# First rows by tiles in two queues, fewer idle products, queries before the first values, and transfers of the early sums and next rows issued at other places

## The chip, the core and the metric

The kernel runs on one core of a Trainium2 chip. The time is device microseconds (us) from start to end of one execution; lower is better. A core has TensorE (PE, products; PEld is its weight load), VectorE (DVE), ScalarE (ACT), GpSimd (POOL) and SyncE (SP, here used to issue DMA transfers). Each engine takes its instructions in order, and they wait for each other through semaphores. Transfers issued by SP and by ACT run on the same 16 DMA engines.

## What is computed

A transformer block on x of 8 sequences, 512 tokens, 256 features, all in float32: attention with 16 heads of 128 (4 groups of keys and values, causal), then a mixture of 64 experts, of which each token takes 6, and a shared expert. Cut to what matters:

```python
def reference(x, wq, bq, wkv, bkv, wo, gate_w, w_gate, w_up, w_down, sh_gate, sh_up, sh_down):
    def attention(x):                                  # x: 8 x 512 x 256
        q = (x @ wq + bq) + pe                         # 4 groups x 4 heads x 128
        k, v = split(x @ wkv + bkv); k = k + pe        # 4 groups x 128 each
        probs = softmax(causal(q @ k.T / sqrt(128)))
        return (probs @ v) @ wo
    def ffn(h):                                        # 4096 tokens, 64 experts, width 176
        w, i = top_k(softmax(h @ gate_w.T), 6)
        y = sum over the 6 of w * ((silu(h @ w_gate[i]) * (h @ w_up[i])) @ w_down[i])
            # of each expert only its first 64 tokens, in the order of tokens
        return y + (silu(h @ sh_gate.T) * (h @ sh_up.T)) @ sh_down.T
    x = x + layernorm(attention(layernorm(x)))
    return x + layernorm(ffn(layernorm(x)))
```

## The kernel before

**Steps.** The main loop runs over k = 0 to 127, a sequence b = k // 16 and a head s = k % 16, and is a pipeline of heads written out by hand: the order of every engine's instructions is the order in which the program calls them. In step k TensorE makes the scores of head k (`scores`, four row tiles of 128, L328), the output product of head k-3 (`project`, L407), the queries of head k+1 (`queries`, L315) and the mixing of head k-2 with the values (`mix`, pav, L390). DVE takes the scores out of PSUM with their mask and row extremum (L332), ACT exponentiates (L335), POOL divides by the row's sum (L345). The scores' PSUM pool has three buffers (`ps_s`, tag "s"), so the fourth tile of a head waits until DVE has evicted the first.

**Turning of the probabilities.** For head k-1, in step k, DVE transposes blocks of 32 x 32 into eb (L361), SP stores them in four transfers to a scratch ex_d (L366), and then reads them back in turned order as et with one transfer of 640 KB (L371). The read waits in SP's queue until the four stores have landed. `turned` also runs, between the stores and the et read, whatever functions the list `readings` holds (L133 to L135 put the turned normalized rows there).

**Sequences.** `prepare(b)` gives the work on a sequence's rows in units: load (`load_x`, L167, one transfer of 512 KB by SP), statistics (`scales`, st_a, L78 to L88, with POOL's power), normalizing (xn, L107), transposing, keys of four groups (pk), values of four row tiles (pv). For sequence 0 the units are called before the loop: keys of group 0, values of tile 0, queries of head 0, and the others in the first steps. For the next sequence the load is called in step s = 6, behind the et read of that step and what a finished sequence stores, the statistics at the end of s = 7, and so on. x has two buffers: rows of b+1 go where those of b-1 were, whose last reader is the normalizing for the feed forward part (xg, L107, step s = 6 in `feed_forward(b-1)`), after a store of them to x1_d (L825, step s = 5).

**Start.** SP loads x of sequence 0, then wkv, biases, the positions, wq in four parts, wo and the shared expert's weights. TensorE makes WARM = 28 products of an identity (L174) before the first transposes (L120).

**Experts and end.** The first five sequences (EARLY) are gathered by expert and run on the way (weights loaded by ACT's queue). In the last steps, `finish_early` finishes their rows: for each of the five, one after the other every four half-steps, it loads the two partial sums y0 and y1 (512 KB each, from y_d, issued by ACT, L711), loads x1 (512 KB, by SP, L726), adds y1 to y0 on POOL (L716), takes statistics (`output`, L78 to L88), scales on ACT (L98), adds x1 on POOL (L702) and stores (L704). The main loop calls it once after the queries and once at a step's end. `last_part` does sequence 7's second half, mixed with what is left of sequence 6 and of `finish_early`. Experts with too many late tokens for the on-the-way buffers are run in a loop after it (L1084), whose count is computed by the kernel; in the profiled execution it was passed without a turn. Behind the loop stand the last products of sequence 7 (L965), which add one late pair's output to PSUM, and `last_output`: statistics, subtraction (L970), scaling and residual (L972), stores (L974).

Each transfer of SP's and ACT's queues ends on one of eight semaphores, taken in turn in the program's order; a transfer waits, on its issuing engine, until the one that had its semaphore before has landed.

Of the kernel before, what the change touches and what calls it, by code (L numbers as in the profile page):

```python
# [11 lines left out]
F32 = mybir.dt.float32  # L12
# [7 lines left out]
P = 128  # L20
B, T, E = 8, 512, 256
NT = B * T
NI = T // P
# [3 lines left out]
NC = E // P  # L27
G, QPG, D = 4, 4, 128
# [7 lines left out]
NEG = -3.0e38  # L36
BIG = 3.0e38
ROW = E + NX
WARM = 28
EARLY = 5  # L40
ET_ROWS = EARLY * T
LROW = ROW + NX
# [2 lines left out]
def sandwich_kernel(ctx, tc, x, wq, bq_t, wkv, bk_t, bv, wo, gate_wt, w_gate, w_up, w_down,  # L45
                    sh_gate_t, sh_up_t, sh_down_t, pe_t, out):
    nc = tc.nc
# [55 lines left out]
    def rows_of(d, first):  # L103
        return d[first : first + T, :].rearrange("(i p) e -> p i e", p=P)
# [19 lines left out]
    readings = []  # L124
# [21 lines left out]
    with ExitStack() as part:  # L146
# [3 lines left out]
        wpool = pool("weights", 1)  # L150
# [9 lines left out]
        def load(ap, shape, name):  # L160
            t = wpool.tile(shape, F32, tag=name, name=name)
            nc.sync.dma_start(out=t, in_=ap)
            return t

        def load_x(b):
            t = p2.tile([P, NI, E], F32, tag="x", name=f"x_{b}")
            nc.sync.dma_start(out=t, in_=x[ts(b, T), :].rearrange("(i p) e -> p i e", p=P))  # L167
            return t

        x_first = load_x(0)  # L170
# [1 line left out]
        warm = ps_s.tile([P, T], F32, tag="s", name="warm")  # L172
        for n in range(WARM):
            nc.tensor.matmul(warm[:, :P], lhsT=ident, rhs=ident, start=True, stop=True)  # L174
        wkv_sb = load(wkv.rearrange("(c p) (g k d) -> p c g k d", p=P, g=G, k=2), [P, NC, G, 2, D], "wkv_sb")
        bk_sb = load(bk_t, [D, G], "bk_sb")
        bq_sb = load(bq_t, [D, NH], "bq_sb")
        pe_sb = load(pe_t, [D, T], "pe_sb")
# [64 lines left out]
        NK = B * NH  # L243
# [309 lines left out]
        table, pairs = {}, {}  # L553
# [153 lines left out]
        def finish(b, tags):  # L707

            ys = [q.tile([P, NI, E], F32, tag=tag, name=f"y{n}_{b}") for n, (q, tag) in enumerate(tags[:2])]
            for k in range(2):  # L710
                nc.scalar.dma_start(out=ys[k], in_=rows_of(y_d, k * (ET_ROWS + CAP) + b * T))  # L711
            yield
            yield
            yield
            x1 = residual(b, *tags[2])
            nc.gpsimd.tensor_add(ys[0], ys[0], ys[1])  # L716
            yield
            yield
            for n, _ in enumerate(output(b, ys[0], x1)):
                yield  # L720
                if n == 1:
                    yield

        def residual(b, q, tag):
            x1 = q.tile([P, NI, E], F32, tag=tag, name=f"x1_{b}")
            nc.sync.dma_start(out=x1, in_=rows_of(x1_d, b * T))  # L726
            return x1
# [168 lines left out]
        def last_part(before, spare):  # L896


            b, xt, sums = B - 1, seqs[B - 1]["x"], po.pop(B - 1)
# [57 lines left out]
            l["part"](py, 0)  # L957
            output6()
            down("late")
            return py, xt, gt, pairs["late"]["dd"]  # L960

        def last_output(py, x1, gt, dd):
            b = B - 1
            for i in range(NI):
                nc.tensor.matmul(py[i // 2][:, i % 2, :], lhsT=gt[:, ts(i, P)], rhs=dd, start=False, stop=True,  # L965
                                 skip_group_check=True)
# [12 lines left out]
        def finish_early():  # L979
            rows = [finish(b, EARLY_TAGS + [[(p1, "xn"), (p2, "xnt")][b % 2]]) for b in range(EARLY)]  # L980
            yield

            for t in range(4 * EARLY + 5):
                for b in range(EARLY):
                    if 0 <= t - 4 * b < 9:
                        next(rows[b])
                yield

# [1 line left out]
        units = list(prepare(0))  # L990
        rest = {"0B": units[9:10], "0D": units[10:11], "1B": units[11:12], "1D": units[5:6], "2B": units[6:7],
                "3B": units[7:8]}
        for u in units[:5] + units[8:9]:
            u()
        queries(0)
        assert len(units) == 12
        behind, ahead = {}, iter(())
        routed, zeroing = experts(), zeros()
# [9 lines left out]
        for k in range(NK):  # L1008
            b, s = divmod(k, NH)
            active = k >= EARLY * NH + 14  # L1010
            scores(k, 0)
            scores(k, 1)
            if 0 <= k - 1 < NK - 2:
                turned(k - 1)
            if twice and not finishing:
# [17 lines left out]
            if finishing:  # L1033
                next(routed, None)
            side(s, "M")
            if s == 6 and b <= EARLY:
                ahead = prepare(b + 1)
                next(ahead)()
            if b <= EARLY and s == 8:
                next(ahead)()  # L1040
            if k >= 2:
# [24 lines left out]
            twice = active and k > EARLY * NH + NH  # L1066
            if twice and not finishing:
                next(routed, None)
            if finishing:
                next(routed, None)  # L1070
            if active and not finishing and "all" in pairs:
                routed, finishing = finish_early(), True
# [11 lines left out]
        with tc.For_i(0, table["rest"], 1) as n:  # L1084
# [17 lines left out]
            down("late")  # L1102
            for i in range(NI):
                nc.tensor.matmul(sums[i // 2][:, i % 2, :], lhsT=gts[-1][:, ts(i, P)], rhs=pairs["late"]["dd"],
                                 start=False, stop=False, skip_group_check=True)
# [62 lines left out]
```

## Time and profile before

| what | us |
|---|---|
| median of 3 runs (lowest, highest) | 1423.16 (1421.56, 1423.8) |
| the profiled execution | 1423.76 |
| its span, first to last instruction | 1422.0 |
| TensorE busy in the span | 1381.9 |
| TensorE waiting for a score tile's eviction by DVE | 10.9 (7 waits) |
| TensorE waiting for et | 5.5 (4 waits) |
| TensorE waiting at the loop before the last products | 2.9 |
| DVE waiting for x | 11.4 (5 waits) |
| mean granted TensorE clock | 0.996 of full |

How to read it: the span is what the trace covers; some 1.8 us of the execution lie around it. A row of the time line has its start, how long the group lasted, engine, line, operation, output and input tile, shape, number of instructions, and in brackets how long the engine stood idle before it and what ended that. A TensorE product in float32 is recorded as passes, two for each product of this kernel. "DMA x<-in_x" as a releaser is a transfer's landing. A wait for several semaphores is put down to the one that came last.

### The profile page before, as it was taken

The numbers are of one execution on the slowest core, as the hardware profiler recorded it, in microseconds if no ns is written. First come the engines' busy times: TensorE is split into PE (matmuls) and PEld (weight loads), VectorE is DVE, ScalarE is ACT, GpSimd is POOL, SyncE is SP. The second block draws the span as 40 slices with busy tenths as digits, with TensorE's granted clock in tenths as the row PEclk, the third lists the DMA queues.
The fourth block names the chain that finished last, engine by engine and source line by source line (L and its number), as shares of the span: only waits on it lengthen the run. The fifth ranks groups of instructions, "written<-read, shape, count | busy, mean of one in ns | idle before, by whom it ended". The sixth has DMA issues, their size and how long they took to land. (4 is left out here: it accounts for less than half of the span.)

```text
span 1422.0 us, 18479 instructions
## 1 busy us (share of the span) xinstructions
PE 1381.9 (97%) x5230; PEld 839.9 (59%) x5230; DVE 887.4 (62%) x3125; ACT 497.5 (35%) x1428; POOL 446.1 (31%) x710
## 2 busy tenths in 40 slices
PE   9999999999999999999999999999999999999996
PEld 5665665666556665666556665655555565555564
DVE  5565577656775576566775577566656545567545
ACT  2332344224342333234432344223343333434421
POOL 2232242213321242113221232124544444445521
PEclk9999999999999999999999999999999999999998
DMA  7675566446763566446663566349998789777711
GB/s 235 187 217 156 153 195 204 138 122 169 220 173 109 150 186 203 127 125 168 202 183 108 148 195 174 110 133 289 296 299 245 227 233 273 191 226 228 231 59 68
DMA packets 166934, 261.45 MB, mean 184 GB/s; under 512 B 17180, under 2 KB 141053, under 8 KB 166829
## 3 DMA queue, kind: packets, MB, share of 16 engines
q1 hardware_dynamic: 132013, 210.96, 50.8%
q10 hardware_dynamic: 28672, 39.85, 9.0%
q0 software_dynamic: 6144, 9.44, 3.4%
q8 instruction: 42, 0.69, 0.2%
q14 instruction: 63, 0.52, 0.1%
HBM read 148.25 MB, written 111.94 MB: 183 GB/s over the span
## 5 line engine op out<-in xcount | busy, mean ns | idle before, releaser
L345 POOL TENSOR_SCALAR e<-e,recip 128x128 f32<-128x128 f32 x508 | 268.4, 572 | 740.0 <-DVE recip L342 727.3
L335 ACT ACTIVATE e<-e,least 128x128 f32<-128x128 f32 (+3 forms) x512 | 285.6, 559 | 361.0 <-DVE least L332 349.0
L328 PE MATMUL psc<-kt,qt 128*128 128x128 f32 (+3 forms) x1024 | 304.8, 436 | 12.9 <-DVE least L332 10.9
L390 PE MATMUL pav<-et,v 128*128 128x512 f32 (+3 forms) x1024 | 298.3, 434 | 5.7 <-DMA et<-ex_d 5.5
L390 PEld LDWEIGHTS pav<-et,v 128*128 128x128 f32 x1024 | 194.2, 191 | 168.5 <-issue 119.3
L332 DVE CUSTOM_DVE_ANT_0 e<-psc,mask 128x128 f32<-128x128 f32 (+3 forms) x512 | 232.5, 479 | 61.3 <-PE psc L328 52.7
L407 PE MATMUL po<-wo_sb,ao 128*128 128x256 f32 x1024 | 243.7, 381 | 2.3 <-ACT ao L110 1.8
L315 PE MATMUL pq<-xnt,wq_sb 128*128 128x512 f32 x512 | 241.1, 593 | 0.3 <-ACT sc L434 0.3
L407 PEld LDWEIGHTS po<-wo_sb,ao 128*128 128x128 f32 x1024 | 193.0, 190 | 74.5 <-issue 41.7
L361 DVE STREAM_TRANSPOSE eb<-e 128x128 f32<-128x128 f32 x756 | 227.8, 364 | 6.9 <-DMA ex_d<-eb 5.9
L110 ACT COPY ao<-pav 128x512 f32<-128x512 f32 x128 | 74.7, 583 | 430.4 <-PE pav L390 412.4
L328 PEld LDWEIGHTS psc<-kt,qt 128*128 128x128 f32 x1024 | 162.2, 191 | 78.0 <-DVE least L332 31.3
L318 DVE SCALAR_TENSOR_TENSOR qt<-pq,bq_sb,pe_sb 128x512 f32<-128x512 f32 x128 | 95.5, 746 | 109.2 <-PE pq L315 109.2
L315 PEld LDWEIGHTS pq<-xnt,wq_sb 128*128 128x128 f32 x512 | 95.9, 190 | 70.2 <-issue 64.0
L342 DVE RECIPROCAL recip<-total 128x4 f32<-128x4 f32 x128 | 22.8, 178 | 121.0 <-ACT e L335 121.0
L335 ACT ACTIVATION_READ_ACCUMULATOR e<-e,least 128x1 f32 x512 | 95.7, 187 | 0.0
L632 POOL DMA_INDIRECT y_d<-dd,idx x32 | 50.8, 1588 | 93.1 <-DMA y_d<-dd,idx 27.5
L285 PE MATMUL pk<-xnt,wkv_sb 128*128 128x512 f32 x128 | 59.3, 594 | 0.2 <-ACT xnt L110 0.2
L296 PE MATMUL pv<-wkv_sb,xnt 128*128 128x512 f32 x128 | 58.1, 592 | 0.0
L298 DVE TENSOR_TENSOR v<-pv,bv_sb 128x512 f32<-128x512 f32 x32 | 22.1, 690 | 45.8 <-PE pv L296 45.8
L288 DVE SCALAR_TENSOR_TENSOR kt<-pk,bk_sb,pe_sb 128x512 f32<-128x512 f32 x32 | 24.0, 750 | 41.4 <-PE pk L285 41.4
L595 PE MATMUL pgu<-wgu,gxt 128*64 128x352 f32 x256 | 43.6, 461 | 0.7 <-issue 0.7
(201 smaller groups left out, 1074.9 us busy)
## 6 DMA issues: line engine op xcount, KB each, us to landing
ex_d<-eb SPq DMA_DIRECT2D x504, 160.0 KB
et<-ex_d SPq DMA_DIRECT2D x126, 640.0 KB
wgu<-in_w_gate ACTq DMA_DIRECT2D x32, 352.0 KB
wgu<-in_w_up ACTq DMA_DIRECT2D x32, 352.0 KB
wd<-in_w_down ACTq DMA_DIRECT2D x32, 352.0 KB
y<-y_d ACTq DMA_DIRECT2D x10, 512.0 KB
x<-in_x SPq DMA_DIRECT2D x8, 512.0 KB
x_d<-x SPq DMA_DIRECT2D x7, 512.0 KB
```

Of the source, the lines that this page charges most:

```text
L110: nc.scalar.copy(dst, src)
L285: nc.tensor.matmul(pk, lhsT=wkv_sb[:, c, g, 0, :], rhs=s["xnt"][:, c, :], start=c == 0, stop=c == NC - 1)
L296: nc.tensor.matmul(pv, lhsT=s["xnt"][:, c, ts(i, P)], rhs=wkv_sb[:, c, :, 1, :], start=c == 0, stop=c == NC - 1)
L315: nc.tensor.matmul(pq, lhsT=wq_sb[h // QPG][:, c, ts(h % QPG, D)], rhs=seqs[b]["xnt"][:, c, :], start=c == 0, stop=c == NC - 1)
L318: nc.vector.scalar_tensor_tensor(qt, pq, bq_sb[:, h : h + 1], pe_sb, ALU.add, ALU.add)
L328: nc.tensor.matmul(psc[:, :w], lhsT=l["qt"][:, ts(i, P)], rhs=seqs[b]["kt"][h // QPG][:, :w], start=True, stop=True)
L332: nc.vector.tensor_tensor_reduce(out=e, in0=psc[:, :w], in1=mask[:, T - w :], scale=-1.0 / math.sqrt(D), scalar=BIG, op0=ALU.add, op1=ALU. ...
L335: nc.scalar.activation(e, e, AF.Exp, bias=l["least"][:, i : i + 1], scale=-1.0, accum_out=l["total"][:, i : i + 1])
L345: engine.tensor_scalar(e, e, recip[:, n : n + 1], 1.0, ALU.mult, ALU.mult)
L361: nc.vector.transpose(blocks.rearrange("p c j t -> p j c t"), l["e"][i][:, js[0] * P : (js[-1] + 1) * P].rearrange("p (j c t) -> p j c t", ...
L390: nc.tensor.matmul(pav[:, :, j:, :], lhsT=seqs[b]["v"][:, j, ts(g, D)], rhs=l["et"][:, :, AT[j] : AT[j] + NI - j, :], start=j == 0, stop=j ...
L407: nc.tensor.matmul(po[b][i // 2][:, i % 2, :], lhsT=ao[:, ts(i, P)], rhs=wo_sb[:, h, :], start=h == 0 and i % 2 == 0, stop=h == NH - 1, sk ...
```

## The change

- Sequence 0's x is loaded in four transfers of one row tile each, on SP and ACT in turn; wkv in two, one on SP and one on ACT. WARM is 14.
- The queries of head 0 are made before the values of tile 0.
- The load of the next sequence's rows goes through `readings`: in step s = 6 SP issues it between the ex_d stores and the et read of that step. It waits there for the x1_d store and for xg, which in the program's order stand before and after it.
- `finish`: y0 in one half-step, y1 in the next, x1 in the one after these; POOL's sum in four instructions, one a row tile; the store one half-step earlier. The last half-step's call at k = 127 is left out, so that what it did (scaling and adding of the fifth sequence) is done by `last_part`.
- The last products stand before the loop, in `last_part`.

```diff
-WARM = 28
+WARM = 14
         def load_x(b):
             t = p2.tile([P, NI, E], F32, tag="x", name=f"x_{b}")
-            nc.sync.dma_start(out=t, in_=x[ts(b, T), :].rearrange("(i p) e -> p i e", p=P))
+            rows = x[ts(b, T), :].rearrange("(i p) e -> p i e", p=P)
+            if b:
+                nc.sync.dma_start(out=t, in_=rows)
+                return t
+
+            for i in range(NI):
+                (nc.sync, nc.scalar)[i % 2].dma_start(out=t[:, i, :], in_=rows[:, i, :])
             return t
...
-        wkv_sb = load(wkv.rearrange("(c p) (g k d) -> p c g k d", p=P, g=G, k=2), [P, NC, G, 2, D], "wkv_sb")
+        wkv_sb = wpool.tile([P, NC, G, 2, D], F32, tag="wkv_sb", name="wkv_sb")
+        for c in range(NC):
+            (nc.sync, nc.scalar)[c].dma_start(out=wkv_sb[:, c], in_=wkv[ts(c, P), :].rearrange("p (g k d) -> p g k d", g=G, k=2))
...
             for k in range(2):
                 nc.scalar.dma_start(out=ys[k], in_=rows_of(y_d, k * (ET_ROWS + CAP) + b * T))
-            yield
-            yield
-            yield
+                yield
             x1 = residual(b, *tags[2])
-            nc.gpsimd.tensor_add(ys[0], ys[0], ys[1])
-            yield
-            yield
-            for n, _ in enumerate(output(b, ys[0], x1)):
-                yield
-                if n == 1:
-                    yield
+            yield
+            for i in range(NI):
+                nc.gpsimd.tensor_add(ys[0][:, i, :], ys[0][:, i, :], ys[1][:, i, :])
+            yield
+            yield
+            yield from output(b, ys[0], x1)
...
             down("late")
-            return py, xt, gt, pairs["late"]["dd"]
-
-        def last_output(py, x1, gt, dd):
+            for i in range(NI):
+                nc.tensor.matmul(py[i // 2][:, i % 2, :], lhsT=gt[:, ts(i, P)], rhs=pairs["late"]["dd"],
+                                 start=False, stop=True, skip_group_check=True)
+            return py, xt
+
+        def last_output(py, x1):
             b = B - 1
-            for i in range(NI):
-                nc.tensor.matmul(py[i // 2][:, i % 2, :], lhsT=gt[:, ts(i, P)], rhs=dd, start=False, stop=True,
-                                 skip_group_check=True)
...
-            for t in range(4 * EARLY + 5):
+            for t in range(4 * EARLY + 4):
                 for b in range(EARLY):
-                    if 0 <= t - 4 * b < 9:
+                    if 0 <= t - 4 * b < 8:
                         next(rows[b])
...
-        for u in units[:5] + units[8:9]:
+        for u in units[:5]:
             u()
         queries(0)
+        units[8]()
...
             scores(k, 1)
+            if s == 6 and b <= EARLY:
+                ahead = prepare(b + 1)
+                readings.append(next(ahead))
             if 0 <= k - 1 < NK - 2:
                 turned(k - 1)
...
-            if s == 6 and b <= EARLY:
-                ahead = prepare(b + 1)
-                next(ahead)()
...
-            if finishing:
+            if finishing and k < NK - 1:
                 next(routed, None)
```

In the loop behind, the same products of a further turn end with stop=True instead of False.

More of the change, by code (lines that the diff above doesn't have):

```diff
@@ L711, in finish @@
                 nc.scalar.dma_start(out=ys[k], in_=rows_of(y_d, k * (ET_ROWS + CAP) + b * T))
+                yield
+            x1 = residual(b, *tags[2])
+            yield
+            for i in range(NI):
+                nc.gpsimd.tensor_add(ys[0][:, i, :], ys[0][:, i, :], ys[1][:, i, :])
             yield
             yield
-            yield
-            x1 = residual(b, *tags[2])
-            nc.gpsimd.tensor_add(ys[0], ys[0], ys[1])
-            yield
-            yield
-            for n, _ in enumerate(output(b, ys[0], x1)):
-                yield
-                if n == 1:
-                    yield
+            yield from output(b, ys[0], x1)
         def residual(b, q, tag):
@@ L1104, in sandwich_kernel @@
                 nc.tensor.matmul(sums[i // 2][:, i % 2, :], lhsT=gts[-1][:, ts(i, P)], rhs=pairs["late"]["dd"],
-                                 start=False, stop=False, skip_group_check=True)
+                                 start=False, stop=True, skip_group_check=True)
             for b in range(EARLY, B - 1):
```

## The prediction

> **What bounds the kernel now.** I read the page first: which engine is full, and whether it is full all the time.
>
> ```profile
> PE 1381.9 (97%) x5230; PEld 839.9 (59%) x5230; DVE 887.4 (62%) x3125; ACT 497.5 (35%) x1428; POOL 446.1 (31%) x710
> ```
>
> TensorE is busy in 97% of the span, so a change can only win where TensorE stands still, where it works slowly, or at the two ends. The second view is who TensorE waited for (us in total, times, longest):
>
> ```profile
> PE psc L328 <- DVE least L332: 10.9, 7, 2.5
> PE pav L390 <- DMA et<-ex_d: 5.5, 4, 1.9
> PE py L965 <- SPq L1084: 2.9, 1, 2.9
> ...
> PE po L407 <- ACT ao L110: 1.8, 1, 1.8
> ```
>
> These are few, long waits, and asked by window they lie in known places: 6.91 us of the first row are four waits, one in each of the sequences 1 to 4 (TensorE stands still at 222.5, 379.0, 535.8 and 692.9 us for 1.46, 1.73, 1.62 and 2.10 us). The rest lies in the last 150 us. The third view is the time line of the start:
>
> ```profile
> 1.87 9.37 PE L174 MATMUL warm<-ident 128*128 128x128 f32 x56 [1.87 <-POOL ident masks.py:199]
> 4.87 1.41 DVE L78 BATCH_NORM_STATS2 st_a<-x 128x6 f32<-128x256 f32 x4 [2.40 <-DMA x<-in_x]
> 7.91 1.38 DVE L107 TENSOR_SCALAR xn<-x,mv_a,rs_a 128x256 f32<-128x256 f32 x4 [1.15 <-POOL rs_a L88]
> 11.08 1.04 PE L120 MATMUL pt_a<-ident,xn 128*128 128x128 f32 x8
> ...
> 18.61 2.43 PE L328 MATMUL psc<-kt,qt 128*128 128x128 f32 x8 [0.84 <-DVE qt L318]
> ```
>
> The rows are normalized at 9.29 us, but the idle products keep TensorE until 11.1: they are the bound there. The fourth is the same around one of the four waits, DVE and then SP:
>
> ```profile
> 210.44 1.84 DVE L107 TENSOR_SCALAR xg<-x,mv_f,rs_f 128x256 f32<-128x256 f32 x4
> 221.85 1.41 DVE L78 BATCH_NORM_STATS2 st_a<-x 128x6 f32<-128x256 f32 x4 [1.99 <-DMA x<-in_x]
> ```
> ```profile
> 213.53 0.34 SPq L371 DMA_DIRECT2D et<-ex_d  x1
> 216.16 0.46 SPq L167 DMA_DIRECT2D x<-in_x  x1
> ```
>
> The next rows are asked for at 216.16 and land at 221.8; DVE stands at their statistics for 1.99 us, the scores behind them are late in leaving PSUM, and TensorE stops.
>
> **Start.** (a) Each of the four x tiles has its own transfer. The last still lands near 4.84 (from 3.5 us on all 16 DMA engines are full in the trace, so a second queue adds no bandwidth), but three tiles' statistics are done by then: only one of four, 0.41 us, comes after it. Statistics end at about 5.25 instead of 6.28: 1.0 us. The chain behind (aggregates, POOL's power of 1.03 us, normalizing) then ends at about 8.25.
>
> (b) 14 products instead of 28. Here a rule speaks against the change. In the trace the 56 passes (two a product) have two speeds. The table by stretches, asked for line L174 alone, shows it in the count of passes (us, length, TensorE busy and passes, weight loads, granted clock, share and rate of the DMA; the clock has no record before 7.9 us, and 1.00 there is a default):
>
> ```profile
> 6.00:8.00 2.00, 2.00 (x12) 2.00 (x11) 1.00 1.07 371
> 8.00:10.00 2.00, 2.00 (x21) 2.00 (x20) 1.00 0.90 244
> ```
>
> A pass starts every 0.2125 us until 7.8 and every 0.111 us after. The Trainium skill (page "TensorE: Matmul & The Clock Gate", Part 1) says that the array runs at half clock until it was busy for one free-running window of about 3.4 us, and goes back after an idle one. The row agrees in kind, but took 6 us, since the first window had begun before the products. By the row, 28 slow passes last 1.87 + 28 x 0.2125 = 7.8 to 8.0 us, just to the rows' arrival and to the end of that window: the transposes follow at full speed, at 7.95 instead of 11.08 less one pass, so 3.1 us earlier, of which (a) is a condition. By the rule, with the window elsewhere, the half clock may last to 12.1, and the transposes, keys and part of the queries (3 to 4 us of work) take about 2 us more, some 0.4 of it behind the transfer below. I take the row and keep the 2 us for the range.
>
> (c) Queries before the values. The first scores waited 0.84 us for DVE's qt; now four passes of values (1.71 us) lie over that 0.75 us eviction: -0.84. But the queries need wq's first part, which lands at 11.46 us in the trace; the keys now end at 9.2 + 1.8 = 11.0, so TensorE waits about 0.4. The bytes ahead of wq are the same. Its issue now also waits for an x tile (a transfer takes over the semaphore of the one eight before it), at 4.5 instead of 3.9 us, while the engines are still full with wkv. Sum of the start: 3.1 + 0.84 - 0.4 = **3.5 us**, from 1.5 (half clock) to 4.2. ScalarE's three issues (1.4 us) come before its table load; it is first needed at 8.5.
>
> **Next rows.** The load goes ahead of the et read in SP's queue, and now waits there for the old rows' last reader, DVE's xg. That ends at 212.28, 368.78, 525.56 and 682.66; the et reads, which wait for the ex_d stores to land, are issued at 213.53, 369.48, 526.40 and 683.52. So the load fits into SP's own wait, 0.7 to 1.25 us before it ends, for 0.4 to 0.9 us of issue, and rows land about 3.9 us earlier than now; DVE wanted them 2.0 to 2.6 us earlier. All four TensorE waits go: **6.9 us**. Behind the load are et and through it the mixing two steps later: it has 0.79 to 1.65 us to spare at these four places (landing of et to pav's start), and 512 KB at the 370 GB/s of the start's trace take 1.4 us, most of them before et's own data would begin: 0.2 to 0.7 us late, inside the spare time. If half of it were not, 4 x 0.4 = 1.6 us come back. Sequences 0 and 5 had no such wait: nothing.
>
> **Last sequences.** (d) At the last step the fifth sum's four ScalarE scalings stood before ao:
>
> ```profile
> 1359.36 2.08 ACT L98 ACTIVATE y<-y,shift_y,rs_y 128x256 f32<-128x256 f32 x4 [2.37 <-POOL shift_y L697]
> 1361.34 0.56 ACT L110 COPY ao<-pav 128x512 f32<-128x512 f32 x1
> ```
>
> TensorE's 1.76 us wait for it goes. The scalings and POOL's four sums (2.77 us) come after the last head instead; POOL is then about 0.5 us late for rs_o, which DVE and the transposes wait for: net 1.2.
>
> (e) y0 and y1 (512 KB each) come half a step apart and x1 one step earlier. Now they come with an output store in one burst of 2 MB, and the ex_d stores behind them land late (issued from 1332.88, landed at 1342.16); two mixings wait 1.91 and 1.59 us for it. With half the burst these should land some 4 us earlier. But stores still wait for a semaphore that a y transfer holds, at new places, where other reads have 1.4 to 2.5 us to spare. Between a gain of 3.5 and as much of new waits I take +2.0, as the bytes in front are halved. y1 lands later, but POOL's sums follow at least 11 us after its new issue, and it took 7.0 to 10.2.
>
> (f) POOL's sum is cut into four (4 x 0.69 for 2.35 us). DVE met it once:
>
> ```profile
> 1288.29 2.34 POOL L716 TENSOR_TENSOR y<-y,y 128x1024 f32<-128x1024 f32 x1
> ```
> ```profile
> 1288.55 2.13 DVE L443 TENSOR_SCALAR xg<-sc,grecip 128x64 f32<-128x64 f32 x1
> ```
>
> Its sister rows take 0.24 us. "SBUF — State Buffer" of the Trainium skill (the single rule on the shared ports) has the pair locked for a whole instruction. Shorter locks let DVE in between, but three more such DVE instructions follow, each of which can meet the next piece: 0 to 1.9, I take 0.3. Sum of the last sequences: 1.2 + 2.0 + 0.3 = **3.5 us**, from -2 to 7.
>
> **End.** The last products stood behind the empty loop:
>
> ```profile
> 1407.30 0.37 ACT L110 COPY dd_late<-pd_late 128x256 f32<-128x256 f32 x1 [2.85 <-PE pd_late L621]
> ...
> 1410.21 3.27 PE L965 MATMUL py<-dd_late,gt 128*128 128x256 f32 x8 [2.95 <-SPq L1084]
> ...
> 1413.52 0.76 DVE L78 BATCH_NORM_STATS2 st_y<-py 128x6 f32<-128x256 f32 x2 [0.95 <-PE py L965]
> ```
>
> They now start at 1407.7 and take 1.99 us, as their like before (they ran at half clock after the pause: 3.27). The loop's exit is set by sequence 6's output landing at 1409.16 and leaves DVE free at 1409.9; with TensorE done at 1409.7 this moves to 1410.2. Four statistics of 0.41 us end at 1411.9 instead of 1414.28: **2.4 us**, 1.0 if every engine waits for TensorE's slow row of semaphore checks.
>
> **Sum.** 3.5 + 6.9 + 3.5 + 2.4 = 16.3 us. The profiled execution took 1423.76 (span 1422.0 and 1.8 around it), 0.6 over the median; the same 16.3 from the median of 1423.16 give **1406.9 us**.
>
> **Rivals.** (1) *Half clock at the start*: speaks for it the rule above and a fall to half clock elsewhere (the last products); against it that TensorE is busy from 1.87 to 8.9 without a break, two windows nearly. Start 1.5: 1408.9. (2) *The last sequences only exchange their waits*: for it the semaphore places, against it the halved burst. -1 instead of 3.5: about 1411.5. (3) *Slower*: SP stands at the next rows' load, because DVE is late with xg, and et and everything behind it in SP's queue are late, at five places (sequence 0's et has 1.70 us to spare). The other gains stay, so it decides only when et is late by 16.3/5 + 1.45 = 4.7 us at each, and gives more than 1426 at 5.3. For it: SP takes its instructions in order. Against it: xg ended 0.7 us or more before et's issue in all four. About 1427. (4) *No change*: TensorE's waits come back elsewhere, as the scores behind DVE. DVE is at 62%, and stood still for the time that is taken away: little for it.
>
> **How the numbers follow.** Forecast 0.63 (its own range 1402 to 1411), rival 1 0.12, rival 2 0.17, rival 3 0.04, rival 4 0.04. A measurement of this kernel tells about 0.2% (2.8 us) from no change. The first three are faster: 0.92; same 0.04; slower 0.04. The range from 1401 (ends of the gains: 4.2, 6.9, 7, 2.6, and a clock fall before the last 160 us avoided) to 1415 (1.5, 5.3, 0, 1.5) holds the first three.
>
> **What would show it.** Right: the transposes of the first rows near 8 us and scores near 14.8; no DVE wait for x after the first rows; no TensorE wait at the loop; last products of 2 us. Wrong: first keys at 0.43 us a pass doubled to 0.85, pav waiting for et of the heads 21, 37, 53, 69 (mixed two steps after), new pav waits after 1270 us, or ScalarE standing at a y1 issue.

## The result

The changed kernel takes **1412.18 us** (median of four runs, 1408.62 to 1414.8), the kernel before 1423.48 beside it: a ratio of **0.9919, 95% interval 0.9892 to 0.9946**. By the ratio it is faster by 11.5 us; the forecast was 16.3 us and 1406.9 us. The time lies inside the range of 1401 to 1415, but above the forecast's own 1402 to 1411 and near the 1411.5 of the second rival, whose reason is not what happened. That it lies inside is partly luck: the range was kept wide for half clock and for exchanged waits, and what came in their place was late weights at the start. A repetition on another occasion gave 1409.95 against 1424.3, ratio 0.9913 [0.9891, 0.9935].

The profiled execution took 1414.8 us (span 1413.1), the slowest of its four. Its page and its waits of TensorE (us in total, times, longest), to be held against the same two views of before:

```profile
PE 1380.6 (98%) x5202; PEld 836.6 (59%) x5202; DVE 889.3 (63%) x3125; ACT 497.9 (35%) x1428; POOL 448.4 (32%) x725
```
```profile
PE ptx L592 <- DVE ht L113: 3.0, 1, 3.0
PE psc L336 <- DVE least L340: 2.9, 3, 1.4
PE pav L398 <- DMA et<-ex_d: 2.9, 3, 1.8
PE psg L764 <- DMA xt<-exr_d: 2.4, 4, 0.8
PE pq L323 <- DMA wq_sb<-in_wq: 2.3, 1, 2.3
...
PE pk L293 <- DMA wkv_sb<-in_wkv: 1.5, 1, 1.5
```

The scores' waits for DVE fell from 10.9 to 2.9 us, the wait for the loop and ScalarE's ao are gone from the list. Three kinds of wait are new or larger: for xt (0.2 before), and for the two weights of the start. The time line of the start shows the last two:

```profile
1.88 5.23 PE L180 MATMUL warm<-ident 128*128 128x128 f32 x28 [1.88 <-POOL ident masks.py:199]
3.64 1.41 DVE L78 BATCH_NORM_STATS2 st_a<-x 128x6 f32<-128x256 f32 x4 [1.17 <-DMA x<-in_x]
...
7.15 1.73 PE L120 MATMUL pt_a<-ident,xn 128*128 128x128 f32 x8
...
10.35 1.95 PE L293 MATMUL pk<-xnt,wkv_sb 128*128 128x512 f32 x4 [1.47 <-DMA wkv_sb<-in_wkv]
...
14.58 2.40 PE L323 MATMUL pq<-xnt,wq_sb 128*128 128x512 f32 x4 [2.27 <-DMA wq_sb<-in_wq]
...
16.77 3.20 PE L304 MATMUL pv<-wkv_sb,xnt 128*128 128x512 f32 x4
...
19.81 1.46 PE L336 MATMUL psc<-kt,qt 128*128 128x128 f32 x6
```

Up to the transposes it goes better than forecast: they begin at 7.15, and end 3.2 us earlier than before. Then the key and value weights, which landed at 7.47 us before, land at 10.41, and the queries' first weights at 14.53 instead of 11.46. The scores begin at 19.81, 1.2 us *later* than before. The long pv row is a fall of the clock to half, which the table by stretches shows (us, length, busy and instructions of PE, PEld, DVE, ACT, POOL, then the granted clock, share and rate of the DMA):

```profile
14.00:16.00 2.00, 1.42 (x4) 0.70 (x5) 0.00 (x0) 0.00 (x0) 0.00 (x0) 1.00 0.85 319
16.00:18.00 2.00, 2.00 (x4) 0.94 (x3) 0.75 (x1) 0.00 (x0) 0.00 (x0) 0.50 0.97 333
```

Where the time went, stage by stage, comes from the starts of each head's first scores in two traces. The table says how many us a kernel is ahead of the profile of before at that point; the last row is the end of the span. The second column is the profile of the changed kernel's repetition, the third a version of experiment 1.

| head | changed | changed, again | old loads | old loads, again |
|---|---|---|---|---|
| 0 | -1.20 | 1.64 | 3.03 | 3.03 |
| 76 | 3.93 | 7.31 | 6.40 | 8.09 |
| 116 | 0.72 | 5.95 | 5.43 | 6.37 |
| 127 | 4.82 | 10.35 | 12.99 | 14.30 |
| end | 8.95 | 14.45 | 17.04 | 18.19 |

So in the changed kernel the start failed, the next rows (heads 0 to 76) gave 5.1 and 5.7 us, something unforeseen took 1.4 to 3.2 between 76 and 116, the last sequences gave over 4, the end about 4 (with ao, which stands behind head 127). Falls of the clock are in these numbers: before has one between heads 116 and 127, the changed kernel's first profile one there, one near 1060 us and one at the start, its repetition none.

### The profile page after: what moved, and what is told of

Its sections match the earlier page's. It is cut to its first block, busy times and chain, and to the rows that moved or that the text cites. A ratio compares the mean times of both kernels' runs of the same rounds, so it can differ in the third digit from the quotient of the medians.

```text
span 1413.1 us, 18469 instructions
## 1 busy us (share of the span) xinstructions
PE 1380.6 (98%) x5202; PEld 836.6 (59%) x5202; DVE 889.3 (63%) x3125; ACT 497.9 (35%) x1428; POOL 448.4 (32%) x725
## 5 line engine op out<-in xcount | busy, mean ns | idle before, releaser
L323 PEld LDWEIGHTS pq<-xnt,wq_sb 128*128 128x128 f32 x512 | 95.8, 190 | 72.8 <-issue 63.5
```

What stands on the lines that cost most here:

```text
L323: nc.tensor.matmul(pq, lhsT=wq_sb[h // QPG][:, c, ts(h % QPG, D)], rhs=seqs[b]["xnt"][:, c, :], start=c == 0, stop=c == NC - 1)
```

## The experiments

Each is shown as its edit, the expectation on record, and the result. Times of landing are read from the trace's semaphore events.

**1. The start's loads.** Four kernels: the changed one again; the weights whole in SP's queue; all six pieces in SP's queue; all loads of the start as before, with the fewer products and the queries ahead of the values kept ("old loads").

> The changed kernel once more, unaltered, for what repeats. If the late key and value weights belong to the change (two queues), they land near 10.3 us again, the keys start near 10.4 and the first scores near 19.8 or, where the clock does not fall, near 18.1. If that one execution merely had slow memory, they land near 7.5, keys start near 9.1 and scores near 15 to 16. DVE's 3.0 us for ht near 1056 us: back at 1.7 or less if it was the execution's, 3.0 again if it is the change's. Whole: 0.989 to 0.995 of the kernel before.

```
# weights whole
-        wkv_sb = wpool.tile(...)
-        for c in range(NC):
-            (nc.sync, nc.scalar)[c].dma_start(out=wkv_sb[:, c], ...)
+        wkv_sb = load(wkv.rearrange(...), [P, NC, G, 2, D], "wkv_sb")
```

> The key and value weights as one transfer in SP's queue again, x still by tiles in two queues. Theory 1 (the second queue lets the small vectors, pe and bv run beside the weights, which therefore land late): they land near 7.5 us, keys start near 9.0, wq's first part lands near 11.5 to 12.5, scores start near 15 to 16.5, 3 to 4.5 us earlier than in the changed kernel, and the whole is about 1408 us. Theory 2 (x by tiles takes up semaphores, so that wq is asked for late, and it decides): wq's first part still lands at 14 us or later and scores start at 18 to 20; whole unchanged within 1 us. Theory 3 (slow memory in that one execution): like the repetition of the changed kernel within 1 us.

```
# one queue
-                (nc.sync, nc.scalar)[i % 2].dma_start(out=t[:, i, :], in_=rows[:, i, :])
+                nc.sync.dma_start(out=t[:, i, :], in_=rows[:, i, :])
...
-            (nc.sync, nc.scalar)[c].dma_start(out=wkv_sb[:, c], ...)
+            nc.sync.dma_start(out=wkv_sb[:, c], ...)
```

> All six transfers of x and of the key and value weights in SP's queue, none on ScalarE's. Theory 1: as with the weights whole, they land near 7.7 (six issues of 0.43 us by one engine put the last at 3.3 us, still ahead of the data), scores near 15.5 to 17. Theory 2: weights near 7.7, but wq's first part at 14 us or later, as the count of transfers is the same as in the changed kernel, and scores at 18 or later.

```
# old loads: weights whole, and
-            if b:
-                nc.sync.dma_start(out=t, in_=rows)
-                return t
-            for i in range(NI):
-                (nc.sync, nc.scalar)[i % 2].dma_start(out=t[:, i, :], in_=rows[:, i, :])
+            nc.sync.dma_start(out=t, in_=rows)
```

> All loads as in the kernel before, with the fewer products and the queries ahead of the values. The rows' statistics end near 6.3, normalized rows near 9.3, transposes end near 9.5, keys 9.9 to 11.7, wq's first part at 11.5, scores near 16.0: 2.6 us earlier than in the kernel before, if the clock is full by then. If 14 products end too soon for the clock (TensorE then stands from about 7.8 until rows come at 8.3 to 9.3), keys and queries take up to 2 us more and scores start near 18. Theory 1 and 2 expect the same here; theory 3 too, less what its memory does.

| kernel | weights issued, landed | wq's first part landed | scores | ratio to before |
|---|---|---|---|---|
| before | 1.28, 7.47 | 11.46 | 18.61 | |
| changed | 1.71, 10.41 | 14.53 | 19.81 | 0.9919 [0.9892, 0.9946] |
| changed, again | 1.71, 10.07 | 13.39 | 16.97 | 0.9913 [0.9891, 0.9935] |
| weights whole | 1.71, 10.08 | 13.03 | 16.61 | 0.9914 [0.9897, 0.9930] |
| one queue | 2.65 and 3.12, 8.16 | 13.54 | 18.81 | 0.9909 [0.9892, 0.9925] |
| old loads | 1.28, 7.46 | 11.21 | 15.58 | 0.9882 [0.9865, 0.9899] |

The lateness repeats, so it is the change's (theory 3 falls). With the weights as one transfer in one queue it is as large, 10.08: theory 1, that the second queue lets the small vectors and pe run beside the weights, falls too. Theory 2 does not fit "weights whole" either, where wq's issue at 4.89 stands 8 us before its landing. With the old loads the weights are back at 7.46, the rows after the transposes have no wait for a weight, and the scores start 3.03 us ahead of before:

```profile
8.36 1.73 PE L120 MATMUL pt_a<-ident,xn 128*128 128x128 f32 x8 [1.26 <-DVE xn L107]
...
10.33 1.98 PE L286 MATMUL pk<-xnt,wkv_sb 128*128 128x512 f32 x4 [0.24 <-ACT xnt L110]
...
12.15 1.88 PE L316 MATMUL pq<-xnt,wq_sb 128*128 128x512 f32 x4
...
15.58 2.32 PE L329 MATMUL psc<-kt,qt 128*128 128x128 f32 x8
```

This is the time line of the old loads' second profile (the first has the same starts). The scores of "changed" and "one queue" hold a fall of the clock as well (at 16.01 and 14.70 us). None of the three theories was right: what the profiles with late weights share is that x is cut, and that the weights are *issued* later. Two further kernels part these.

**2. Cut, or late issue.**

```
# x in halves, one queue
-            nc.sync.dma_start(out=t, in_=rows)
+            for i in range(1 if b else 2):
+                half = slice(0, NI) if b else ts(i, NI // 2)
+                nc.sync.dma_start(out=t[:, half, :], in_=rows[:, half, :])
```

> As with all loads of the kernel before and 14 products, but x in two transfers of two tiles each, both in SP's queue. If cutting x alone makes the bytes behind it slow, as with four transfers: the key and value weights land 0.5 us or more later than 7.5, wq's first part later than 11.9, and scores start at 16 or later. If it was the number of issues in front of the weights: weights near 7.6, statistics end near 5.6 instead of 6.25, scores near 15.0 instead of 15.6.

Weights issued at 1.78 landed at 9.17, wq at 13.47, scores at 18.75 (span 1408.6, one execution). Cutting in two is enough; it does not say whether by the cut or by the 0.5 us that the second issue of x puts in front of the weights.

```
# x whole, small vectors ahead of the weights
-        wkv_sb = load(wkv.rearrange(...), ...)
         bk_sb = load(bk_t, [D, G], "bk_sb")
         bq_sb = load(bq_t, [D, NH], "bq_sb")
+        wkv_sb = load(wkv.rearrange(...), ...)
```

> Loads of the kernel before with x whole, but the two small vectors bk and bq (10 KB) issued ahead of the key and value weights, so that these are issued at 2.2 us, as in the kernels with x cut, instead of 1.3. If the late issue (engines run dry between x and the weights) makes the bytes behind slow: weights land at 8.5 or later, wq's first part at 12.5 or later. If cutting x does: weights land near 7.7, wq near 11.5, scores near 15.7.

Here x is whole and lands at 4.80 as ever, and only 10 KB go ahead of the weights. They land at 9.75, and wq at 13.93, though wq is issued at 3.75, earlier than the 3.87 of before:

```profile
2.29 0.43 SPq L162 DMA_DIRECT2D wkv_sb<-in_wkv  x1
...
13.97 1.98 PE L316 MATMUL pq<-xnt,wq_sb 128*128 128x512 f32 x4 [1.68 <-DMA wq_sb<-in_wq]
```

So cutting x is not needed for it. In all eight profiles in which the weights were issued at 1.28 us, they landed between 7.45 and 7.91 and wq's first part between 10.9 and 12.0; in all six with an issue at 1.71 or later, the weights landed between 8.16 and 10.41 and wq between 13.0 and 14.5. Half a microsecond of issue goes with some 2 us of wq's landing. Two things stay joined in these runs: in the eight, one transfer (x) is issued ahead of the weights, in the six it is two to four. And the delay does not grow with the time of issue: "one queue" issues them last, at 2.65, and they land first of the six, at 8.16. So it is shown that what is issued ahead of the weights delays them; whether by the later time or by the number of transfers is not.

It is not a later start: the weights' first packets of 4096 bytes begin between 3.57 and 3.80 us in the five profiles with x cut and between 3.81 and 3.89 in the eight (at 4.25 in the kernel with the vectors first). What the packets show is a slower pace behind it: with the early issue, in the stretch from 4 to 5 us, in which x ends, the 16 engines are full and a packet of 4096 bytes takes 160 ns, 436 GB/s in all (before). With x in halves the same stretch is 7.4 of 16 engines busy and 127 GB/s, and the packets take 240 to 250 ns until 6 us; after that the engines are some 2 us apart (bk's packets, all within one microsecond before, are spread over 6 to 9 us), and a transfer has landed only when the last engine is through. Why packets are slower and engines drift apart was not found. The same stretch, before and then with x in halves (the last two numbers are the share and rate of the DMA; the share counts packets that start in it, so it can pass 1):

```profile
4.00:5.00 1.00, 1.00 (x6) 1.00 (x6) 0.13 (x1) 0.00 (x0) 0.54 (x3) 1.00 1.10 436
```
```profile
4.00:5.00 1.00, 1.00 (x6) 1.00 (x6) 1.00 (x4) 0.00 (x0) 0.54 (x3) 1.00 0.47 127
```

In the kernel with the vectors first the packets are quick at once (162 ns), but only 36 of them start in that microsecond, where before has 89; both effects need not have one cause.

**3. What the products and the order are worth.** The old loads with 28 products again:

```
-WARM = 14
+WARM = 28
```

> The fastest version with 28 idle products again. It parts the start's 3.0 us into products and order. Transposes begin when the products end, near 10.1 to 11.1 us (10.1 in two profiles with 28 products, 11.1 in a third), scores near 16.7 to 17.7: products worth 1.1 to 2.1 us, order (queries ahead of the values) the remaining 0.9 against 17.7 to 18.6. If the products are worth nothing, scores near 15.6.

```profile
9.96 1.04 PE L120 MATMUL pt_a<-ident,xn 128*128 128x128 f32 x8
...
16.49 2.32 PE L329 MATMUL psc<-kt,qt 128*128 128x128 f32 x8
```

Scores at 16.49 instead of 15.58: without x by tiles, 14 products fewer are worth 0.91 us (one execution with 28 against two with 14), not the 3.1 of steps (a) and (b) together. The rows are late in the old loads: they are normalized from 7.89 on, and the transposes wait 1.26 us for them. And the 11.08 us in the profile of before, where its transposes began, was a late case: in three other profiles with 28 products they begin at 9.96, 10.09 and 10.16, since the clock became full earlier. The two of these that keep the old order start the scores 7.54 us after the transposes, this one 6.53, so the order is worth 1.0 us (forecast 0.84 less 0.4).

**4. The next rows alone**, in the kernel before:

```
+            if s == 6 and b <= EARLY:
+                ahead = prepare(b + 1)
+                readings.append(next(ahead))
...
-            if s == 6 and b <= EARLY:
-                ahead = prepare(b + 1)
-                next(ahead)()
```

> The kernel before with the next rows' load moved ahead of the et read, nothing else. The forecast's step: the four stops of 1.46 to 2.10 us gone and nothing new, 6.9 us by head 76, ratio 0.995. The changed kernel's trace instead: 4.5 to 5.7 us by head 76, because the turned rows that the shared expert reads (xt) now come last, 0.5 to 1.0 us late at each sequence, and et of head 21 or 37 up to 0.6 late; ratio 0.996 to 0.997. Rival 3 (SP stands at the load) would give et late by over 2 us at each of five places and no gain.

1419.62 against 1425.72, ratio 0.9957 [0.9942, 0.9972], so 6.1 us with 4.0 to 8.3. The interval holds the forecast's 6.9 too, so the times alone do not say that the step was over-sized; the traces do. In this kernel's trace (its slowest execution of six) the gain from head 0 to 76 is 3.3 us, where the changed kernel had 5.1 and 5.7 and the old loads 3.4 and 5.1. The four stops are gone in each. In their place stand these, here of the changed kernel:

```profile
224.47 1.95 PE L764 MATMUL psg<-xt,sg_sb 128*128 128x512 f32 x4 [0.80 <-DMA xt<-exr_d]
...
375.81 2.42 PE L398 MATMUL pav<-et,v 128*128 128x512 f32 x8 [0.65 <-DMA et<-ex_d]
...
380.99 1.96 PE L764 MATMUL psg<-xt,sg_sb 128*128 128x512 f32 x4 [0.60 <-DMA xt<-exr_d]
```

xt is the turned rows of the shared expert. In the trace of before it landed at 224.71, 381.53, 538.62 and 695.75, and its reader began at 224.96, 381.73, 538.76 and 695.98: it was just in time only because TensorE had stood still for the scores. And et of head 37 is late by what the load puts ahead of it (5.25 us from issue to landing, 4.33 before).

**5. The load behind et**, with the old loads of the start:

```
             while readings:
                 readings.pop()()
             l["et"] = p2.tile(...)
             nc.sync.dma_start(out=l["et"]..., in_=ex...)
+            while loads:
+                loads.pop()()
...
-                readings.append(next(ahead))
+                loads.append(next(ahead))
```

> All loads of the start as in the kernel before, the other parts as in the changed kernel, and the next rows' load just behind the et read in SP's queue instead of just ahead of it. If the rows' 512 KB ahead of et are what makes et of heads 21, 37, 53 and 69 land 5.7 us after its issue instead of 4.3: et is back at 4.2 to 4.6 us, no mixing wait at these heads, the rows still land 2 us or more before DVE wants them, and head 76 is 0.5 to 2.5 us earlier than with the load ahead (3.4 us gained from head 0 to 76 there, with one fall of the clock). If et is late for another reason, its 5.7 us stay. xt waits of 0.5 to 1.0 us remain in both.

1413.56 against 1425.72, ratio 0.9923 [0.9899, 0.9946]: not better but, by its median, worse than with the load ahead of et (0.9882 and 0.9890). et is back (4.36, 4.33, 4.23 and 4.42 us), as expected. What was not expected is xt:

```profile
222.05 1.96 PE L759 MATMUL psg<-xt,sg_sb 128*128 128x512 f32 x4 [1.79 <-DMA xt<-exr_d]
...
379.20 3.50 PE L759 MATMUL psg<-xt,sg_sb 128*128 128x512 f32 x4 [2.11 <-DMA xt<-exr_d]
...
537.71 1.95 PE L759 MATMUL psg<-xt,sg_sb 128*128 128x512 f32 x4 [1.80 <-DMA xt<-exr_d]
...
693.11 1.96 PE L759 MATMUL psg<-xt,sg_sb 128*128 128x512 f32 x4 [0.40 <-DMA xt<-exr_d]
```

6.1 us in four waits, and nothing gained from head 0 to 76 (-0.2 us); one of the waits comes with a fall of the clock (3.50 for four passes that take 1.96). The load now runs just ahead of the stores that xt is read from: at the first of these places the last of them lands at 218.59, 5.9 us after its issue, where in the old loads it lands at 216.15, after 4.8. In SP's order one of two readers pays for these 512 KB, and ahead of et is the cheaper place.

**6. The early sums alone**, in the kernel before (y0, y1 half a step apart, x1 earlier, POOL's sum in four, nothing at the last head):

```
             for k in range(2):
                 nc.scalar.dma_start(out=ys[k], ...)
-            yield
-            yield
-            yield
+                yield
             x1 = residual(b, *tags[2])
-            nc.gpsimd.tensor_add(ys[0], ys[0], ys[1])
-            yield
-            yield
-            for n, _ in enumerate(output(b, ys[0], x1)):
...
+            yield
+            for i in range(NI):
+                nc.gpsimd.tensor_add(ys[0][:, i, :], ys[0][:, i, :], ys[1][:, i, :])
+            yield
+            yield
+            yield from output(b, ys[0], x1)
...
-            if finishing:
+            if finishing and k < NK - 1:
                 next(routed, None)
```

> The kernel before with only the early sums' new order (y0 and y1 half a step apart, x1 a step earlier, POOL's sum in four pieces, nothing at the last head). The forecast's step: 3.5 us (1.2 for ao, 2.0 for the stores behind the smaller burst, 0.3 for the port), ratio 0.9975, within -2 and 7 us. If the waits are only exchanged (rival 2): -1 to 1 us, the ao wait of 1.76 us gone and as much of new mixing waits. From the changed kernel's trace: the wait for the scores' eviction near 1290 falls from 2.5 to 1.4, one of two mixing waits is gone (1.6), ao's wait is gone (1.8): 4.5 us; if the clock does not fall near 1264 us as it did in the kernel before, 1.5 us more that are not the change's.

1419.09 (20 runs) against 1425.72, ratio 0.9958 [0.9942, 0.9973]: 6.0 us, with 3.8 to 8.3. Its trace gains 5.7 us from head 116 to 127, of which about 1.5 are the fall of the clock at 1264 us that this profile of before has and this one does not. Rival 2, waits that are only exchanged, falls.

**7. The last products behind the loop again**, in the old loads, beside the old loads once more:

> All loads of the start as in the kernel before, the other parts as in the changed kernel, once more and with more rounds: the fastest version found. Ratio 0.987 to 0.990 of the kernel before, as the first time (0.9882), where the changed kernel has 0.991 to 0.992. Weights near 7.5, wq's first part near 11.3, scores near 15.6 again if whole x is what keeps the weights early.

```
# the last products moved from last_part to last_output
-            for i in range(NI):
-                nc.tensor.matmul(py[i // 2][:, i % 2, :], lhsT=gt[:, ts(i, P)], rhs=pairs["late"]["dd"], ...)
-            return py, xt
+            return py, xt, gt, pairs["late"]["dd"]
```

> The same with the last eight products behind the empty loop again, as in the kernel before. The forecast's step: 2.4 us longer, ratio 0.0017 higher, TensorE waiting about 2.9 us for the loop and DVE's last statistics 2.4 us later after the last head's scores. If it was worth nothing: less than 1 us.

1408.32 (ratio 0.9890 [0.9863, 0.9917]) with the products ahead of the loop, 1410.63 (0.9910 [0.9884, 0.9936]) behind it: 2.8 us in the ratios, 2.3 in the medians; the intervals overlap, so the times alone do not show it. The traces do. From head 127's first scores to the end of the span it takes 69.4 to 69.8 us in all ten profiles with the products ahead of the loop, and 72.8 and 73.0 in the two that have the early sums' new order and the products behind it. From head 127's first scores to the end of DVE's last four statistics it takes 61.8 us with the products ahead of the loop and 65.2 behind it; 1.8 of these 3.4 us are half clock in the products (behind the loop first, then ahead of it):

```profile
1396.08 3.78 PE L963 MATMUL py<-dd_late,gt 128*128 128x256 f32 x8 [3.03 <-SPq L1083]
```
```profile
1392.25 1.99 PE L959 MATMUL py<-dd_late,gt 128*128 128x256 f32 x8 [0.47 <-ACTq L1083]
```

## Why the prediction was right, and where it was wrong

**Start (a), wrong; this is the step that failed.** The statistics came as forecast (they end at 5.04, forecast 5.25). "The bytes ahead of wq are the same" is true and did not help: the same bytes landed 3 us later with the weights issued 0.43 us later and behind more transfers. The step put the extra issues at nothing since the engines were full "from 3.5 us on" in the trace of before. In the changed kernel they are not filled alike: between 4 and 5 us they move 201 GB/s, where before moved 436. So the start gave -1.2 and 1.6 us in two profiles instead of 3.5. In the old loads it gives 3.03.

**Start (b), over-sized**: 0.9 us in experiment 3, where x is whole; the 3.1 of the forecast took a late case of the clock as its base. (c) was 1.0 instead of 0.4. Rival 1, half clock at the start, was seen in one profile, the second kernel of experiment 7: the clock rose at 5.84 us and fell again from 9.25 to 12.67, the keys took 2.84 instead of 1.98, and the scores were 1.59 ahead instead of 3.03 (0.4 of this is x, which landed at 5.27 there). The fall in the changed kernel's own profile (16.01 us) has another cause, the wait for wq.

**Next rows, right in mechanism, over-sized**: 5.1 and 5.7 us for 6.9. All four stops went and SP did not stand at the load (rival 3), which at the first of the four places was issued at 212.59, 0.6 us ahead of the et read, and landed at 216.56:

```profile
212.59 0.40 SPq L169 DMA_DIRECT2D x<-in_x  x1
213.20 0.34 SPq L379 DMA_DIRECT2D et<-ex_d  x1
```

The term that was missing is the next thing late behind the stop: xt, with 0.14 to 0.25 us to spare in the trace of before. Its waits took 2.4 us in the changed kernel's profile. The loss named for et came at one of four places.

**Last sequences, right in mechanism, somewhat under-sized.** (d) ao's 1.76 us went; from head 127 to the start of the last products it is 61.7 us before and 57.8 after, and less the 2.5 of the loop's wait 1.4 of them arrived (forecast 1.2). (e) One mixing wait of two went (1.59), the other stayed (1.91 before, 1.84 after, 1.56 in the repetition): forecast 2.0, measured 1.7 to 1.9 in the changed kernel; over all twelve profiles with the new order such waits of over 0.25 us take between 0 and 1.8 us there, against 3.5 before. The stores behind the burst land 10.2 us after the et read ahead of them, 12.2 before: 2 us earlier, not 4. Ahead of the other wait the trace shows the semaphore that was named: an ex_d store behind the one of 1310.0 us was held to 1314.93, until y0's transfer, which had its semaphore, landed at 1314.92. But the old loads hold their store in the same way (to 74.5 us behind head 116's scores, in the changed kernel 76.9) and have no such wait, so the hold alone does not make it. (f) was 1.1 us and not 0.3:

```profile
1285.82 0.32 DVE L451 TENSOR_SCALAR xg<-sc,grecip 128x64 f32<-128x64 f32 x1
1286.05 2.78 POOL L724 TENSOR_TENSOR y<-y,y 128x256 f32<-128x256 f32 x4
...
1286.31 0.52 DVE L451 TENSOR_SCALAR xg<-sc,grecip 128x64 f32<-128x64 f32 x1
...
1287.01 0.51 DVE L451 TENSOR_SCALAR xg<-sc,grecip 128x64 f32<-128x64 f32 x1
...
1287.70 0.50 DVE L451 TENSOR_SCALAR xg<-sc,grecip 128x64 f32<-128x64 f32 x1
```

Every following DVE instruction meets a piece, but each loses only 0.27 us to it, against 1.9 us to the whole; the four take 1.85 us where they took 2.93, and TensorE's wait fell by just these 1.08 us, from 2.52 to 1.44. Each of the three ends 0.05 us after a piece of POOL's does (pieces end at 1286.78, 1287.47 and 1288.15), as the one of before ended 0.05 us after the whole. That agrees with the rule of the Trainium skill ("SBUF — State Buffer", section "Who interferes with whom"), by which the pair of ports is held for a whole instruction and the other engine waits: here DVE gets it between two instructions of POOL.

**End, right.** The products follow the end of dd_late's copy within 0.1 us and take 1.99 us:

```profile
1401.09 0.37 ACT L110 COPY dd_late<-pd_late 128x256 f32<-128x256 f32 x1 [2.85 <-PE pd_late L629]
...
1401.52 1.99 PE L966 MATMUL py<-dd_late,gt 128*128 128x256 f32 x8 [0.47 <-ACT dd_late L110]
...
1403.90 1.43 DVE L78 BATCH_NORM_STATS2 st_y<-py 128x6 f32<-128x256 f32 x4 [5.14 <-PEq L1090]
```

From head 127 to the end the changed kernel gains 4.1 us, of which 1.4 are ao's: 2.7 for a forecast of 2.4. Against the two profiles of experiment 7's comparison that have the products behind the loop it is 3.0 to 3.6; there the eight products took 3.5 and 3.8 us at half clock, 3.3 before.

**The stretch from head 76 to 116** had no term, and lost 1.4 to 3.2 us in the two profiles. Most of the larger loss is one wait for ht (an expert's hidden values, turned) near 1056 us: 3.0 us in the changed kernel's profile, 1.67 in its repetition, 1.65 before, and in the others from 1.3 to 3.0, with a fall of the clock behind it in four profiles. The rows alone have 3.0 as well, the early sums alone 1.3. That it comes with the next rows' move is possible: the stretch ranges from 0.3 us won to 3.8 lost in the twelve profiles that have the move, and loses 0.1 in the one that has not, the early sums alone. It varies by 1.9 us between two executions of the changed kernel, and the cause stays open.

**The sum.** The old loads reach 1406.93 and 1408.32 in two comparisons (ratios 0.9882 and 0.9890, so 15.7 to 16.8 us), close to the forecast's 16.3. That closeness is luck: the start without its failed step gave 3.0 of 3.5, the next rows 3.4 and 5.1 of 6.9, the stretch without a term took 1.0 and 1.7, and heads 116 to 127 gave 7.6 and 7.9, of which some 1.7 are the fall of the clock that this profile of before has there. The changed kernel with its two queues is slower than this by 4.4 us in the ratios and 3.0 in the medians of the comparison that had both; the intervals overlap by a little. The start's traces account for 1.4 to 4.2 us of it. Another 3.2 to 3.8 lie between heads 116 and 127, where the two kernels run the same instructions; this part was not explained, and the twelve profiles with the new order of the early sums gain between 4.0 and 7.9 us there. "Old loads" has the lowest median in both of its comparisons.

## What to carry to other kernels

A load at the start is worth what its issue order makes it: count the transfers issued in front of each large one, not only the bytes. Before a stop is booked as a gain in full, look for what lands within a few tenths of a microsecond behind it; it will be the next wait. Two kernels that differ by 0.3% are better told apart by the start times of the same step in their traces, stage by stage, than by their medians; but take two traces of each, since one stage of unchanged code moved by several microseconds here.

## What was not expected of the hardware

**The clock falls for less than a full stop.** The records of the granted clock step on a grid of 3.413 us in each profile. Laid on that grid, TensorE's busy share of each window says what comes next, in 14 profiles, up to 1395 us and leaving out the first 2 us: of the nine windows with a share of 0.42 or less, three of them at the start, every one was followed by half clock for 3.4 us or more; of those with 0.61 or more none; between 0.43 and 0.60 some were (at 0.49, 0.51, 0.53, 0.56, 0.57 and 0.60) and most were not. A stop of 2.0 us is enough if it lies in one window (the old loads at 370.4 us, share 0.42), and one of 2.5 us did nothing where the window that it hit most kept a share of 0.48 (before, at 1289.5). The first of these, window by window (columns as in the table by stretches of the result; 1.44 of 3.42 us are 0.42, and the clock is the third number from the end):

```profile
369.18:372.60 3.42, 1.44 (x4) 0.37 (x3) 2.31 (x9) 0.67 (x2) 2.06 (x4) 1.00 0.96 346
372.60:376.01 3.41, 3.41 (x6) 1.67 (x7) 0.38 (x5) 0.00 (x0) 1.02 (x1) 0.50 0.63 185
```

The Trainium skill ("TensorE: Matmul & The Clock Gate", Part 1 and "Why this matters for your kernels") speaks of an idle window and of stops above about 3 us; the runs put the limit at about half a window. By these records a fall at full work costs about 1.7 us, half of its 3.41, and which stop meets one changes from run to run. In the 25 runs of before beside experiments 4 to 6, and in the 20 of the early sums alone, the time goes with the mean granted clock of the run (correlations -0.84 and -0.85), so falls of the clock are most of the 3 us (standard deviation) by which runs of one kernel differ there.

**The late weights** of experiment 2: issued 0.43 to 1.0 us later, they landed 1.7 to 2.9 us later than in the profile of before in five profiles; in the sixth (one queue, weights in two parts, issued 1.4 to 1.8 us later) only 0.7 later, with bv and wq behind them 2.1 to 2.5 later.
